# Work moved off ScalarE and VectorE in two attention layers: keys and values evicted by two engines, averages and edge columns on GpSimd, and a written-out ending

## The chip, the cores and the metric

The kernel runs on one core of a Trainium2 chip. The metric is the device time of one execution in microseconds, the median of three runs. The engines are named as in the profile: PE is TensorE's matrix multiplication and PEld its weight load, DVE is VectorE, ACT is ScalarE, POOL is GpSimd, and SP is SyncE, which here only issues DMAs. An "L" with a number is a line of the kernel before.

## What is computed

Four layers work in turn on `x` of shape (2, 128, 64, 64), all in fp32. The first is a sequence layer with a state-space scan, the second an attention with 3x3 convolutions for queries, keys and values; the change does not touch either. The third is an attention over all 4096 positions of each picture:

```python
q = einsum('dc,nci->ndi', wq, xf) + bq      # keys and values alike, with wk and wv
scores = einsum('nci,ncj->nij', q, k)
attn = softmax(scores, axis=-1)
out = einsum('ncj,nij->nci', v, attn)
return gamma[0] * out + x
```

The fourth is an attention between four scales of the same picture, at each position:

```python
for i, scale in enumerate((1, 2, 4, 8)):
    if scale > 1:
        xs = x.reshape(b, c, h//scale, scale, w//scale, scale).mean(axis=(3, 5))
        f = bilinear_resize(conv3x3(xs, conv_w[i], conv_b[i]), h, w)
    else:
        f = conv3x3(x, conv_w[i], conv_b[i])
# q, k, v of the 4 features; 8 heads of 16 channels; softmax over the 4 scales
res = (softmax(q k / 4) v) @ attn_out_w.T + attn_out_b + features
normed = (res - mu) * rsqrt(var + 1e-5) * ln_g + ln_b
out = einsum('bchw,oc->bohw', normed of the 4 scales, fus_w) + fus_b
```

## The kernel before, in words

The 128 channels lie on the partitions. The order of the instructions is written out by hand: each engine executes its instructions in the order of the code, and waits where an operand or a buffer is not ready. So an instruction that waits also holds up what is behind it on its engine.

**The attention layers.** One loop with a counter `now` runs over four "runs" of 128 steps, `runs = [(layer, batch)]`; runs 2 and 3 are the third layer of the network (called the second attention layer here). A run is processed in groups of 256 queries, `score` (L754, L759) writing the products of queries and keys `pq` into a pair of PSUM banks and copying them to SBUF while it takes their maximum, later steps of the same queue doing the exponential on ScalarE (L769), a transposition (L784 on DVE, then copies and DMAs to `pt`, L791 to L795) and the product with the values (`po`, L804). At step 0 of a run `keys` computes the 4096 keys in four chunks; at step 13 `values` does the same, and turns each chunk by eight TensorE transpositions (`turned`, `pvt` L714, copied by ScalarE at L716). In runs 2 and 3 `chunks` fills a pair of banks `pp` by two products (L683), and one ScalarE instruction, `put` (L592), adds the bias and writes the 1024 elements to SBUF. `pp` and `pq` share two buffers of two banks each. `query(r, 0)`, the first 256 queries, stands behind `keys`: a product `pqq` and a ScalarE `put`.

**The last layer.** There are 16 items, 8 of each batch, each of 512 positions by 4 scales. Its loop `period(n)` works on four items at once: the features of item n+2, the scores of item n+1, the weighting and mixing of item n, and the normalising and fusing of item n-1. In the order of the code a period has these steps:

- four slots, `ti` = 0 to 3. In each: `product` on DVE (L1157), `weights` on PE (`pw`, L1199), `scores` on PE (L1164), `weighted` on DVE (`ov`, L1206). In slot 0 also `normalise` (L1257) and `fuse` (`pfus`, L1264) of the item before; in slot 1 `add_ov` on POOL (L1210).
- two `add_ov` on DVE (L1210), the softmax on DVE and ACT (L1174 to L1192),
- `mix_out`: four times a pair of products `po` (L1219, L1220) and two ScalarE evictions, the square `sq` and the centred value `cen` (L1221, L1222),
- `variance` (`pva`, L1228, then three ScalarE instructions, L1233 to L1236), `newton` (`nt`, `rs`: DVE L1241, ACT L1242, DVE L1243), `factors` (`prs`, L1250), which spreads the result over the channels for the `normalise` of the next period.

`pw` and `prs` share one buffer of four PSUM banks; `psc`, `pva` and `pfus` share one bank; `po`, `pf`, `pqkv` and `pcs` share three.

`extra` places three things of a batch in slots of a period. `means` computes the averages of 2x2, 4x4 and 8x8 positions: two additions per scale on DVE (L1053, L1054), a `memset` on POOL (L1056), and ScalarE scales the sum into a padded tile (L1057). `coarse_conv` is the 3x3 convolution at that scale (`pcs`, L1069). `columns` interpolates along the rows: a difference `df` (L1085), two edge copies (L1088, L1089), one DVE instruction for each phase (L1092: 2, 4 and 8 of them), copies of the first and last row (L1095, L1096), and for the two coarser scales the difference of rows `di` (L1100). `features` builds the upsampled features of an item from them on POOL (L1124 to L1134). Batch 0 has them ahead of the loop. For batch 1, `means` stands behind the softmax of period 2, the convolutions in periods 3 and 4, and `columns` behind the softmax of period 5. The two last calls of the loop are period 15, in which only the old items have work, and period 16, which normalises and fuses item 15.

Of the kernel before, what the change touches and what calls it, by code (L numbers as in the profile page):

```python
# [6 lines left out]
F32 = mybir.dt.float32  # L7
AF = mybir.ActivationFunctionType
ALU = mybir.AluOpType
# [58 lines left out]
def tile_conv_seq(ctx: ExitStack, tc, x, consts, vecs, wemb, wlay, wconv, wdt, wqkv, wsmall, wms, out):  # L68
# [47 lines left out]
    with tc.manual_schedule(), ExitStack() as s:  # L116
# [474 lines left out]
        def put(dst, src, bias):  # L591
            nc.scalar.activation(dst, src, AF.Identity, bias=bias)  # L592

        def bias(r, which):
            return v1("b" + "qkv"[which] + "12"[runs[r][0]])
# [91 lines left out]
        def chunks(r, which, to):  # L687

            for cc in range(NCC):
                dst = to(cc)  # L690
                if runs[r][0]:
                    pp = pss.tile([P, 2, CH], F32, name="pp", tag="s")
                    for i in range(2):
                        dense(r, which, (2 * cc + i) * CH, CH, pp[:, i, :])
                    put(dst.rearrange("p (a f) -> p a f", a=2), pp, bias(r, which))
                else:
                    pp = products(which)
                    if cc + 1 < NCC:
                        fetch(cc + 1)
                    outputs(*pp, [dst[:, i * QG : (i + 1) * QG] for i in range(4)], bias(r, which))  # L700
# [36 lines left out]
        def query(r, grp):  # L737
            ps = psq.tile([P, QG], F32, name="pqq", tag="q")
            dense(r, 0, grp * QG, QG, ps)
            q = sta["q", r, grp] = spa.tile([P, QG], F32, name="q", tag="q", bufs=5)  # L740
            put(q, ps, bias(r, 0))
# [157 lines left out]
        for now in range(NALL + LAG + 10):  # L899
            r, u = divmod(now, NU)  # L900
            w = now % 8
            if now < NALL:
                if u == 0:
                    if r == 2:
                        wm = wbig.tile([P, NS, 9, C], F32, name="wm", tag="wbig")
                        nc.sync.dma_start(wm, wms)
                    if r:
                        keys(r)
                    if runs[r][0]:
                        query(r, 0)  # L910

                r4, cc = divmod((now + 16) // 32, NCC)
                v = (now + 16) % 32
                if now >= 16 and r4 < B:
                    if v == 0 and r4 and cc:
                        fetch(cc)
                    elif v == 0:
                        ahead = inputs(r4, cc)
                    if v < 6 and not (r4 and cc):
                        for f in ahead[2 * v : 2 * v + 2]:  # L920
                            f()
                    if v == 6 and r4 and cc == 0:
                        keep(0)
                    if v == 14:
                        queries(r4, cc)
                        if r4 and cc == 0:
                            load(1, HI)

                if r == 0 and u >= 32:
                    v = u % 32  # L930
                    if v == 0:
                        other = inputs(1, u // 32)
                    if v < 6:
                        for f in other[2 * v : 2 * v + 2]:
                            f()
                    if v == 6:
                        keep(u // 32)
                score(r, u)
                if runs[r][0]:
                    if w == 2 and u // 8 + 1 < NU // 8:  # L940
                        query(r, u // 8 + 1)
                elif u == 1 and r:
                    load(2, LO), load(2, HI)
                    fetch(0)
                elif u == LAG:
                    load(0, LO), load(0, HI)
                    if r == 0:
                        load(1, LO)
# [23 lines left out]
    with ExitStack() as s, tc.manual_schedule():  # L972
# [70 lines left out]


        def means(b):
            prev, off = xt[:, b], 1
            for si in range(1, NS):
                sc_ = SCALES[si]
                hh = H // sc_
                t1 = sp.tile([P, 2 * hh, hh], F32, name=f"t1_{si}", tag="prod", bufs=6)  # L1050
                sm = sp.tile([P, hh, hh], F32, name=f"sm_{si}", tag=f"fl{si}")
                e = off + 2 * hh
                nc.vector.tensor_tensor(t1, prev[:, off:e, off:e:2], prev[:, off:e, off + 1 : e : 2], ALU.add)  # L1053
                nc.vector.tensor_tensor(sm, t1[:, 0 : 2 * hh : 2, :], t1[:, 1 : 2 * hh : 2, :], ALU.add)  # L1054
                xs = coarse["xs", si] = sp.tile([P, hh + 2, hh + 2], F32, name=f"xs_{si}", tag=f"xs{si}")
                nc.gpsimd.memset(xs, 0.0)  # L1056
                nc.scalar.activation(xs[:, 1 : hh + 1, 1 : hh + 1], sm, AF.Copy, scale=1.0 / (sc_ * sc_))  # L1057
                prev, off = sm, 0

        def coarse_conv(si, r0):  # L1060
# [15 lines left out]
            else:  # L1076
                nc.scalar.activation(dst, src, AF.Identity, bias=v1("conv_b3", si))

        def columns(si):

            sc_ = SCALES[si]
            hh, half = H // sc_, sc_ // 2
            fl = coarse["fl", si]
            df = sp.tile([P, hh, hh - 1], F32, name=f"df_{si}", tag="prod", bufs=6)
            nc.vector.tensor_tensor(df, fl[:, :, 1:], fl[:, :, : hh - 1], ALU.subtract)  # L1085
            lo = sp.tile([P, hh + 2, W], F32, name=f"lo_{si}", tag=f"lo{si}")
            mid = lo[:, 1 : hh + 1, :]
            nc.vector.tensor_copy(mid[:, :, :half], fl[:, :, 0:1].to_broadcast([P, hh, half]))  # L1088
            nc.vector.tensor_copy(mid[:, :, W - half :], fl[:, :, hh - 1 : hh].to_broadcast([P, hh, half]))  # L1089
            for kk in range(half, half + sc_):  # L1090
                end = kk + sc_ * (hh - 2) + 1
                nc.vector.scalar_tensor_tensor(  # L1092
                    mid[:, :, kk:end:sc_], df, (kk + 0.5) / sc_ - 0.5, fl[:, :, : hh - 1], ALU.mult, ALU.add
                )
            nc.vector.tensor_copy(lo[:, 0, :], lo[:, 1, :])  # L1095
            nc.vector.tensor_copy(lo[:, hh + 1, :], lo[:, hh, :])  # L1096
            di = None
            if si > 1:
                di = sp.tile([P, hh + 1, W], F32, name=f"di_{si}", tag=f"di{si}")
                nc.vector.tensor_tensor(di, lo[:, 1:, :], lo[:, : hh + 1, :], ALU.subtract)  # L1100
            low[si] = lo, di


# [169 lines left out]
        def period(n, extra):  # L1273
# [49 lines left out]
                    do(p, newton)  # L1323
                do(r, project, 0, si)
            do(r, project, 1, 0)
            do(p, factors)
            do(r, project, 1, 1)
            more(6)

        means(0)  # L1330
        for r0 in (0, 16):
            coarse_conv(1, r0)
        coarse_conv(2, 0), coarse_conv(3, 0)
        for si in range(1, NS):
            columns(si)
        last = NCH - 3
        extra = {
            (last - 3, 4): [(means, (1,))],
            (last - 2, 1): [(coarse_conv, (1, 0))], (last - 2, 3): [(coarse_conv, (1, 16))],
            (last - 1, 1): [(coarse_conv, (2, 0))], (last - 1, 3): [(coarse_conv, (3, 0))],  # L1340
            (last, 4): [(columns, (si,)) for si in range(1, NS)],
        }
        for n in range(-2, NI + 1):
            period(n, extra)


# [79 lines left out]
```

## Time and profile before

| | |
|---|---|
| median of three runs | 5029.0 us (5028.12 to 5030.46) |
| the profiled execution's own time | 5032.79 us |
| its span, first to last instruction | 5031.0 us |
| granted TensorE clock, mean | 0.948 |
| PE busy | 4671.6 us, 93% of the span |
| DVE busy | 4024.3 us, 80% |
| ACT busy | 2367.4 us, 47% |
| POOL busy | 2309.9 us, 46% |
| keys of run 2 and 3 | from 3230.6 and about 3716 us |
| values of run 2 and 3 | to 3311.7 and 3795.7 us |
| last layer's regular period | 42.4 us from one `pva` to the next |
| last `weighted` to the end | 4995.75 to 5031.0 us |

The profile is of one execution, and every time stamp below is counted from the start of its span. Times of one instruction are from that execution too. In a timeline a line gives the start, the duration, the engine and line, the operation with its output and inputs, and in brackets how long the engine had been idle and what ended the idle time. ACTq and SPq are the DMA issues of these engines. In the list of waits a line gives the instruction that waited, the one that it waited for, the sum of the waits, how often, and the longest one.

### The profile page before, as it was taken

Reading aid. Unit: us, or ns where it says so; the run is one execution under the profiler, and the core shown is the slowest. Engines: PE = TensorE matmul, PEld = TensorE weight load, DVE = VectorE, ACT = ScalarE, POOL = GpSimd, SP = SyncE. Lnnn points to the kernel's source line nnn. Section 1 sums busy time; section 2 is a strip of 40 time slices with the busy share of each in tenths; the row PEclk is TensorE's granted clock in tenths of the full one; section 3 lists DMA queues with packets and bytes.
Section 4 is the critical chain, followed back from the end, with each engine's and each line's share of the span. In section 5 each row is a group of like instructions: output and inputs, shape, how many; then the busy total and the mean of one; then the engine's idle time right before and its main releaser. Section 6 shows DMA issues by size and latency. Waiting matters only on the chain.

```text
span 5031.0 us, 48923 instructions
## 1 busy us (share of the span) xinstructions
PE 4671.6 (93%) x14797; PEld 2244.9 (45%) x14797; DVE 4024.3 (80%) x4284; ACT 2367.4 (47%) x3221; POOL 2309.9 (46%) x1948
## 2 busy tenths in 40 slices
PE   5889999999988899899999999999999999999997
PEld 1222222222222222366667766666666666333332
DVE  6999999999999999788886677667766775767775
ACT  4677777777777777522222222333333332223332
POOL 3777776666777777513332233233333333323331
PEclk8898889988999989899999999999999999999998
DMA  6333333332333333224444344434443442000000
GB/s 162 68 68 69 69 71 71 71 68 63 71 68 68 72 71 70 62 65 108 109 110 126 105 112 110 117 98 110 114 100 97 112 111 70 5 5 7 7 7 7
DMA packets 242343, 386.24 MB, mean 77 GB/s; under 512 B 88592, under 2 KB 88992, under 8 KB 233632
## 3 DMA queue, kind: packets, MB, share of 16 engines
q1 hardware_dynamic: 192928, 315.94, 25.9%
q10 hardware_dynamic: 49152, 67.17, 5.4%
q8 instruction: 118, 1.93, 0.2%
q14 instruction: 145, 1.19, 0.1%
HBM read 101.02 MB, written 13.37 MB: 23 GB/s over the span
## 4 chain that ended last, share of the span: by engine, by line
PE 49%; POOL 24%; issue 12%; DVE 9%; ACT 2%; DMA 2%; SPq 1%; ACTq 0%; DVEq 0%; POOLq 0%
POOL h L410 19%; PE po L804 15%; PE pq L754 15%; PE pa L652 2%; PE pf L1113 2%; DVE tr L784 2%; PE pqkv L1140 2%; POOL dtu L370 1%; PE pw L1199 1%; POOL z L433 1%; PE pb L652 1%; PE pfus L1264 1%; PE psc L1164 1%; PE po L1220 1%; DVE prod L1157 1%
## 5 line engine op out<-in xcount | busy, mean ns | idle before, releaser
L791 POOL COPY pt<-tr 32x512 f32<-32x512 f32 x1024 | 649.0, 634 | 1440.2 <-DVE tr L784 711.7
L407 DVE TENSOR_TENSOR_SCAN h<-da,carry,h 128x512 f32<-128x512 f32 x1024 | 1241.6, 1266 | 59.9 <-ACT da L396 31.0
L410 POOL TENSOR_TENSOR h<-h,cb 128x2048 f32<-128x2048 f32 x256 | 1161.4, 4537 | 20.9 <-POOL carry L409 0.4
L754 PE MATMUL pq<-k,q 128*128 128x512 f32 x2048 | 962.8, 593 | 9.1 <-DVE sc L759 6.8
L804 PE MATMUL po<-pt,vt 128*128 128x256 f32 x4096 | 967.3, 379 | 2.8 <-DMA pt<-tr 2.8
L769 ACT ACTIVATE sc<-sc,nm 128x2048 f32<-128x2048 f32 x256 | 510.5, 1995 | 912.0 <-DVE nm L765 675.4
L759 DVE TENSOR_SCALAR_CACHE_REDUCE sc<-pq 128x1024 f32<-128x1024 f32 x512 | 625.0, 1222 | 366.7 <-PE pq L754 345.4
L804 PEld LDWEIGHTS po<-pt,vt 128*128 128x128 f32 x4096 | 779.1, 190 | 295.6 <-issue 208.3
L396 ACT ACTIVATE da<-dtb,am 128x512 f32<-128x512 f32 x1024 | 681.6, 684 | 231.1 <-DVE h L407 210.2
L389 DVE TENSOR_TENSOR h<-bb,pdu 128x2048 f32<-128x2048 f32 x256 | 581.8, 2273 | 85.8 <-PE py L422 29.3
L784 DVE STREAM_TRANSPOSE tr<-sc 128x2048 f32<-128x2048 f32 x256 | 591.7, 2311 | 63.2 <-DMA pt<-tr 53.9
L422 PE MATMUL py<-h,sel 128*32 128x512 f32 x2048 | 511.4, 643 | 1.6 <-POOL h L410 1.6
L754 PEld LDWEIGHTS pq<-k,q 128*128 128x128 f32 x2048 | 382.8, 190 | 284.8 <-issue 246.1
L383 PE MATMUL pdu<-dtu,fsel 128*128 128x512 f32 x512 | 325.3, 722 | 116.0 <-DVE h L389 113.8
L422 PEld LDWEIGHTS py<-h,sel 128*32 128x32 f32 x2048 | 115.2, 118 | 415.3 <-issue 409.9
L310 PE MATMUL pu<-xn,wu 128*128 128x512 f32 x512 | 246.7, 615 | 2.6 <-ACT xn L300 1.7
L383 PEld LDWEIGHTS pdu<-dtu,fsel 128*128 128x128 f32 x512 | 95.9, 214 | 321.8 <-DVE h L389 199.2
L409 POOL COPY carry<-h 128x4 f32<-128x4 f32 x256 | 47.5, 185 | 395.8 <-DVE h L407 393.9
L1206 DVE TENSOR_TENSOR ov<-v,pw 128x2048 f32<-128x2048 f32 x64 | 146.2, 2285 | 68.6 <-PE pw L1199 68.6
L1140 PE MATMUL pqkv<-f,ws 128*128 128x512 f32 x384 | 189.5, 618 | 3.0 <-DVE prod L1157 2.3
L1210 POOL TENSOR_TENSOR ov<-ov 128x2048 f32<-128x2048 f32 x16 | 72.6, 4536 | 257.7 <-DVE ov L1206 257.7
L370 POOL TENSOR_TENSOR dtu<-dt,u 128x1024 f32<-128x1024 f32 x32 | 75.1, 2346 | 191.9 <-ACT dt L364 191.9
(245 smaller groups left out, 5254.4 us busy)
## 6 DMA issues: line engine op xcount, KB each, us to landing
pt<-tr SPq DMA_DIRECT2D x2048, 64.0 KB, 2.0
dtb<-dt SPq DMA_DIRECT2D x1024, 64.0 KB, 2.0
pt<-tr ACTq DMA_DIRECT2D x1024, 64.0 KB, 2.2
bb<-dr SPq DMA_DIRECT2D x128, 256.0 KB, 4.4
cb<-dr SPq DMA_DIRECT2D x128, 256.0 KB, 4.7
uw<-ufold SPq DMA_DIRECT2D x12, 576.0 KB, 4.3
uw<-dkept SPq DMA_DIRECT2D x20, 288.0 KB, 3.0
xt<-in_x SPq DMA_DIRECT2D x16, 256.0 KB, 4.7
```

Of the source, the lines that this page charges most:

```text
L383: nc.tensor.matmul(pdu, lhsT=four(s_ % 4), rhs=st[i]["dtu"][:, s_ // 4, :], start=True, stop=True)
L389: nc.vector.tensor_tensor(h, st[i]["bc", 0], pdu.unsqueeze(1).to_broadcast([P, 4, CH]), ALU.mult)
L396: nc.scalar.activation(da, st[i]["dtb", s_], AF.Exp, scale=am[items[i][1]][:, j, gg, m : m + 1])
L407: nc.vector.tensor_tensor_scan(h[:, m, :], da, h[:, m, :], carries[b, l][:, j, gg, m : m + 1], ALU.mult, ALU.add)
L410: nc.gpsimd.tensor_tensor(h, h, st[i]["bc", 1], ALU.mult)
L422: nc.tensor.matmul(py[r : r + 32, :], lhsT=sel, rhs=st[i]["h", s_ + k][:, m, :], start=(m == 0), stop=(m == 3), tile_position=(0, r),)
L754: nc.tensor.matmul(pq[:, i, :], lhsT=sta["q", r, grp][:, it * P : (it + 1) * P], rhs=sta["k"][:, at : at + CH], start=True, stop=True)
L759: nc.vector.tensor_scalar(dst, pq, 1.0, None, ALU.mult, ALU.max, accum_out=sta["mx"][:, c2 : c2 + 1])
L769: nc.scalar.activation(sc, sc, AF.Exp, bias=nm, scale=scale, accum_out=sm[:, hh : hh + 1])
L784: nc.vector.transpose(tr, sta.pop(("sc", r, blk, hh)).rearrange("p (t r f) -> p r t f", r=NB, f=32))
L791: nc.gpsimd.tensor_copy(dst, src)
L804: nc.tensor.matmul(sta["po", r, grp], lhsT=sta["vt"][:, jt, :], rhs=rhs, start=(jt == 0), stop=(jt == N // P - 1))
```

## The change

It has four parts. In `chunks` the two banks of a pair are evicted by two instructions, the first by ScalarE and the second by VectorE (a `tensor_scalar` that adds the bias), both into the same destination tile; and the first queries of a run stand ahead of its keys. For batch 1, `means` is done on POOL in whole, with ScalarE's scaling too. `columns` is cut into three parts: for batch 1 the first (difference and edge copies) is done by POOL in slot 3 of period 5, the second (one instruction for each phase) by DVE behind the softmax, where all of it stood before, the third (edge rows and `di`) by POOL behind `mix_out`. And `ending` takes the place of periods 15 and 16: all the weighting of item 15 first, then the factors, normalising and fusing of item 14 (its factors stood in period 14 before), the additions with the last one cut in four by scale, the mixing of item 15, and its normalising cut in four by scale, each quarter with its fusing product.

```diff
@@ -692,7 +692,8 @@
                     pp = pss.tile([P, 2, CH], F32, name="pp", tag="s")
                     for i in range(2):
                         dense(r, which, (2 * cc + i) * CH, CH, pp[:, i, :])
-                    put(dst.rearrange("p (a f) -> p a f", a=2), pp, bias(r, which))
+                    put(dst[:, :CH], pp[:, 0, :], bias(r, which))
+                    nc.vector.tensor_scalar(dst[:, CH:], pp[:, 1, :], bias(r, which), None, ALU.add)
                 else:
                     pp = products(which)
                     if cc + 1 < NCC:
@@ -904,10 +905,10 @@
                     if r == 2:
                         wm = wbig.tile([P, NS, 9, C], F32, name="wm", tag="wbig")
                         nc.sync.dma_start(wm, wms)
+                    if runs[r][0]:
+                        query(r, 0)
                     if r:
                         keys(r)
-                    if runs[r][0]:
-                        query(r, 0)
 
                 r4, cc = divmod((now + 16) // 32, NCC)
                 v = (now + 16) % 32
@@ -1043,6 +1044,8 @@
 
 
         def means(b):
+
+            eng = nc.gpsimd if b else nc.vector
             prev, off = xt[:, b], 1
             for si in range(1, NS):
                 sc_ = SCALES[si]
@@ -1050,11 +1053,14 @@
                 t1 = sp.tile([P, 2 * hh, hh], F32, name=f"t1_{si}", tag="prod", bufs=6)
                 sm = sp.tile([P, hh, hh], F32, name=f"sm_{si}", tag=f"fl{si}")
                 e = off + 2 * hh
-                nc.vector.tensor_tensor(t1, prev[:, off:e, off:e:2], prev[:, off:e, off + 1 : e : 2], ALU.add)
-                nc.vector.tensor_tensor(sm, t1[:, 0 : 2 * hh : 2, :], t1[:, 1 : 2 * hh : 2, :], ALU.add)
+                eng.tensor_tensor(t1, prev[:, off:e, off:e:2], prev[:, off:e, off + 1 : e : 2], ALU.add)
+                eng.tensor_tensor(sm, t1[:, 0 : 2 * hh : 2, :], t1[:, 1 : 2 * hh : 2, :], ALU.add)
                 xs = coarse["xs", si] = sp.tile([P, hh + 2, hh + 2], F32, name=f"xs_{si}", tag=f"xs{si}")
                 nc.gpsimd.memset(xs, 0.0)
-                nc.scalar.activation(xs[:, 1 : hh + 1, 1 : hh + 1], sm, AF.Copy, scale=1.0 / (sc_ * sc_))
+                if b:
+                    nc.gpsimd.tensor_scalar(xs[:, 1 : hh + 1, 1 : hh + 1], sm, 1.0 / (sc_ * sc_), None, ALU.mult)
+                else:
+                    nc.scalar.activation(xs[:, 1 : hh + 1, 1 : hh + 1], sm, AF.Copy, scale=1.0 / (sc_ * sc_))
                 prev, off = sm, 0
 
         def coarse_conv(si, r0):
@@ -1076,28 +1082,35 @@
             else:
                 nc.scalar.activation(dst, src, AF.Identity, bias=v1("conv_b3", si))
 
-        def columns(si):
-
+        def columns(b, si, part):
+
+            eng = nc.gpsimd if b else nc.vector
             sc_ = SCALES[si]
             hh, half = H // sc_, sc_ // 2
             fl = coarse["fl", si]
-            df = sp.tile([P, hh, hh - 1], F32, name=f"df_{si}", tag="prod", bufs=6)
-            nc.vector.tensor_tensor(df, fl[:, :, 1:], fl[:, :, : hh - 1], ALU.subtract)
-            lo = sp.tile([P, hh + 2, W], F32, name=f"lo_{si}", tag=f"lo{si}")
-            mid = lo[:, 1 : hh + 1, :]
-            nc.vector.tensor_copy(mid[:, :, :half], fl[:, :, 0:1].to_broadcast([P, hh, half]))
-            nc.vector.tensor_copy(mid[:, :, W - half :], fl[:, :, hh - 1 : hh].to_broadcast([P, hh, half]))
-            for kk in range(half, half + sc_):
-                end = kk + sc_ * (hh - 2) + 1
-                nc.vector.scalar_tensor_tensor(
-                    mid[:, :, kk:end:sc_], df, (kk + 0.5) / sc_ - 0.5, fl[:, :, : hh - 1], ALU.mult, ALU.add
-                )
-            nc.vector.tensor_copy(lo[:, 0, :], lo[:, 1, :])
-            nc.vector.tensor_copy(lo[:, hh + 1, :], lo[:, hh, :])
+            if part == 0:
+                df = coarse["df", si] = sp.tile([P, hh, hh - 1], F32, name=f"df_{si}", tag="prod", bufs=6)
+                eng.tensor_tensor(df, fl[:, :, 1:], fl[:, :, : hh - 1], ALU.subtract)
+                lo = coarse["lo", si] = sp.tile([P, hh + 2, W], F32, name=f"lo_{si}", tag=f"lo{si}")
+                mid = lo[:, 1 : hh + 1, :]
+                eng.tensor_copy(mid[:, :, :half], fl[:, :, 0:1].to_broadcast([P, hh, half]))
+                eng.tensor_copy(mid[:, :, W - half :], fl[:, :, hh - 1 : hh].to_broadcast([P, hh, half]))
+                return
+            lo = coarse["lo", si]
+            if part == 1:
+                mid, df = lo[:, 1 : hh + 1, :], coarse.pop(("df", si))
+                for kk in range(half, half + sc_):
+                    end = kk + sc_ * (hh - 2) + 1
+                    nc.vector.scalar_tensor_tensor(
+                        mid[:, :, kk:end:sc_], df, (kk + 0.5) / sc_ - 0.5, fl[:, :, : hh - 1], ALU.mult, ALU.add
+                    )
+                return
+            eng.tensor_copy(lo[:, 0, :], lo[:, 1, :])
+            eng.tensor_copy(lo[:, hh + 1, :], lo[:, hh, :])
             di = None
             if si > 1:
                 di = sp.tile([P, hh + 1, W], F32, name=f"di_{si}", tag=f"di{si}")
-                nc.vector.tensor_tensor(di, lo[:, 1:, :], lo[:, : hh + 1, :], ALU.subtract)
+                eng.tensor_tensor(di, lo[:, 1:, :], lo[:, : hh + 1, :], ALU.subtract)
             low[si] = lo, di
 
 
@@ -1323,25 +1336,55 @@
                     do(p, newton)
                 do(r, project, 0, si)
             do(r, project, 1, 0)
-            do(p, factors)
+            if p != NI - 2:
+                do(p, factors)
             do(r, project, 1, 1)
             more(6)
+
+        def ending():
+
+            o, p = NI - 2, NI - 1
+            for ti in range(NS):
+                weights(p, ti)
+                weighted(p, ti)
+                if ti == 1:
+                    add_ov(nc.gpsimd, p, 0, 1)
+            factors(o)
+            normalise(o)
+            fuse(o, range(NS))
+            add_ov(nc.vector, p, 2, 3)
+            a, b = st[p]["ov", 0], st[p].pop(("ov", 2))
+            for si in range(NS):
+                nc.vector.tensor_tensor(a[:, si, :], a[:, si, :], b[:, si, :], ALU.add)
+            for si in range(NS):
+                mix_out(p, si)
+            variance(p)
+            newton(p)
+            factors(p)
+            w = st[p]
+            for si in range(NS):
+                nc.vector.tensor_tensor(w["cen"][:, si, :], w["cen"][:, si, :], w["prs"][:, si, :], ALU.mult)
+                fuse(p, (si,))
 
         means(0)
         for r0 in (0, 16):
             coarse_conv(1, r0)
         coarse_conv(2, 0), coarse_conv(3, 0)
         for si in range(1, NS):
-            columns(si)
+            for part in range(3):
+                columns(0, si, part)
         last = NCH - 3
         extra = {
             (last - 3, 4): [(means, (1,))],
             (last - 2, 1): [(coarse_conv, (1, 0))], (last - 2, 3): [(coarse_conv, (1, 16))],
             (last - 1, 1): [(coarse_conv, (2, 0))], (last - 1, 3): [(coarse_conv, (3, 0))],
-            (last, 4): [(columns, (si,)) for si in range(1, NS)],
+            (last, 3): [(columns, (1, si, 0)) for si in range(1, NS)],
+            (last, 4): [(columns, (1, si, 1)) for si in range(1, NS)],
+            (last, 5): [(columns, (1, si, 2)) for si in range(1, NS)],
         }
-        for n in range(-2, NI + 1):
+        for n in range(-2, NI - 1):
             period(n, extra)
+        ending()
 
 
 # ---- launch: one core ----
```

## The prediction

> **What bounds the kernel now.** I read the page's first line, then a table of busy time by stretch, the list of waits of the last stage, and the timelines around the places that the diff names.
>
> ```profile
> PE 4671.6 (93%) x14797; PEld 2244.9 (45%) x14797; DVE 4024.3 (80%) x4284; ACT 2367.4 (47%) x3221; POOL 2309.9 (46%) x1948
> ```
>
> TensorE is busy for 93% of the span. By stretch it is 543.62 of 560 us in 3230–3790 (a layer-2 attention run), 596.64 of 630 us in 4340–4970 (most of the last layer), but 43.64 of 71 us in 4960–5031. So a change pays where it closes a hole in TensorE, and elsewhere nearly not at all. What holes there are in 4340–4970, from the waits (total us, times, longest):
>
> ```profile
> PEld po L1219 <- ACT cen L1222: 7.7, 2, 7.5
> ...
> PE prs L1250 <- DVE rs L1243: 7.1, 1, 7.1
> ...
> PE po L1219 <- ACT cen L1222: 6.7, 1, 6.7
> ```
>
> Two holes, each once. Period starts tell what they cost: from one `pva` group to the next a regular period takes 42.4 us; the two periods with the holes take 51.1 and 51.6, so 8.7 and 9.2 us are lost. The first hole's timeline (start, duration, instruction, idle before it):
>
> ```profile
> 4406.53 4.62 DVE L1210 TENSOR_TENSOR ov<-ov 128x2048 f32<-128x2048 f32 x2
> ...
> 4417.05 2.25 DVE L1053 TENSOR_TENSOR t<-xt 128x2048 f32<-128x2048 f32 x1
> ...
> 4420.65 1.61 ACT L1057 ACTIVATE xs<-sm 128x1024 f32<-128x1024 f32 x2 [6.70 <-DVE sm L1054]
> ...
> 4423.89 2.07 PE L1219 MATMUL po<-f,kc 128*128 128x512 f32 x2 [6.68 <-ACT cen L1222]
> ```
>
> ScalarE stands at the scaling of `means(1)`, which needs VectorE's averages, and the evictions of `po` (L1221, L1222) queue behind it. The second hole and the lock beside it:
>
> ```profile
> 4585.43 0.61 POOL L1133 TENSOR_TENSOR f<-di,wgt 128x256 f32<-128x256 f32 x1 [1.56 <-DVE di L1100]
> 4585.48 0.60 DVE L1089 COPY lo<-fl 128x32 f32<-128x32 f32 x1
> ...
> 4589.69 0.68 DVE L1241 SCALAR_TENSOR_TENSOR nt<-pva,nt 128x512 f32<-128x512 f32 x1
> ...
> 4591.91 2.09 PE L1250 MATMUL prs<-rs,kc 32*128 32x512 f32 x8 [7.09 <-DVE rs L1243]
> ```
>
> Newton's `nt` was ready at 4582.1 (end of ACT L1236) and waits behind `columns` on VectorE, 4576.38 to 4589.77. The keys of run 2, and the tail:
>
> ```profile
> 3237.23 2.12 ACT L592 ACTIVATE k<-pp,vec 128x1024 f32<-128x1024 f32 x2 [2.34 <-DMA pt<-tr]
> 3238.39 6.11 PE L683 MATMUL pp<-xt,wa 128*128 128x512 f32 x8 [4.18 <-ACT k L592]
> 3244.55 1.11 ACT L592 ACTIVATE k<-pp,vec 128x1024 f32<-128x1024 f32 x1 [1.22 <-PE pp L683]
> 3245.56 0.47 ACT L592 ACTIVATE q<-pqq,vec 128x256 f32<-128x256 f32 x1
> 3246.08 1.98 PE L754 MATMUL pq<-k,q 128*128 128x512 f32 x4 [1.13 <-ACT q L592]
> ```
>
> ```profile
> 4975.04 2.09 PE L1250 MATMUL prs<-rs,kc 32*128 32x512 f32 x8 [4.30 <-DVE rs L1243]
> 4979.54 2.09 PE L1199 MATMUL pw<-at,spread 32*128 32x512 f32 x8 [2.41 <-DVE cen L1257]
> ...
> 5002.81 2.08 PE L1220 MATMUL po<-ov,wc 128*128 128x512 f32 x2 [5.12 <-DVE ov L1210]
> ```
>
> The tail is one chain PE, DVE, PE, with nothing beside it.
>
> **What the Trainium skill says.** "SBUF — State Buffer", section "SBUF: two separate sides": VectorE (two SBUF inputs, or a two-port mode) and a GpSimd operation that reads SBUF share a port pair under an exclusive lock; whichever starts first keeps it for the whole instruction and the other blocks. The trace agrees: the 32-element copies L1089 take 0.20 us alone, 0.60 above behind POOL's 0.61; the L1092 128x56 ones 0.25 alone and 0.77–0.80 when POOL runs; products with one operand in PSUM keep 2.29 us beside POOL's 4.54. "GPSIMD Engine Reference", section 3.1, states 4497 against 2293 ns for an addition of 2048 floats; the rows show 4537 (POOL L1210) and 2.29. "TensorE: Matmul & The Clock Gate", part 1: half clock after some 3.4 us idle. Here the L683 pitch is 0.43 us, and 0.86 after the 4.18 us hole.
>
> **The change part by part.** Nothing before 3230 us is touched. All sums are differences in the profiled execution (span 5031.0 us, execution 5032.79, 1.8 around the span); that execution is 3.8 above the median 5029.0, and I subtract from the median.
>
> *Keys and values of runs 2, 3.* Removed: an ACT eviction of 1.11 us per pair; added: ACT for one bank (0.69, as L1116) and VectorE for the other (0.69–0.73, as L1241 and L1174). VectorE is idle there (14.8 and 14.2 us before the first score). But in the built program VectorE's instruction waits for ScalarE's of the same pair, since both write one tile: 0.69+0.05+0.70 = 1.44 in series against 1.11. Keys: first query first, so q's put (0.47) goes before the keys; third pair at 3237.23+0.47+1.44 = 3239.13 instead of 3238.39 (+0.74); after the fourth pair, though, neither 0.60 of `pqq` nor q's put is left, and the first score needs only the keys' first part. The chain from the third pair to the score shrinks from 7.69 to about 5.9: first score 1.0 earlier. Values: the first `pvt` half reads bank 0 alone, so it starts after 0.69 instead of 1.11; following the four pairs through PE, ACT and DVE I get 1.1 of the 9.84 us (3301.83 to 3311.67). Twice both: 4.2. Bounds: if all 16 series costs lay on the path, 16×0.33 = 5.3 lost; if none, 6 gained. VectorE's values also wait for the tile's last transfers, issued 3304.4, 2.0 us to land, before it needs them.
>
> *Means of batch 1.* Removed: six VectorE sums (5.1 us) and ACT's 1.87 in front of `po`. Added on POOL, after its ov addition that ends 4401.62: 2048 sum 4.54, 1024 sum 2.35 (as L370), memsets 1.6, scaling of 1024 between 2 (as a two-operand row) and 3.4 (L1124's 0.86 per 256), small ones about 4: 15 us in all, needed by `coarse_conv` at about 4447. POOL's features behind it have slack: POOL idles 23.0 us before L1124. Without interference the period would be 42.4 and `pva` at 4418.86 for 4427.60. But the first sum ends at 4406.2 and the second runs 4406.28–4408.63, just where VectorE's two additions stood (4406.53–4411.15). Both sides alternate under the lock: additions end about 4415.4, softmax 4 us later, `pva` about 4421.8. Gain 5.8 to 6.0; bounds 3.5 (one more operation blocked) and 8.7.
>
> *Columns of batch 1.* Only the 14 scalar-tensor-tensors stay on VectorE in slot 4 (7.46 us in the trace); differences, edge copies and `di` (in all 5.9 of 13.4) go to POOL ahead and behind. `nt` runs at 4582.3–4584.8 instead of 4589.69, `prs` at 4584.8–4587.3 for 4591.91. The remaining wait is under 3.4 us, so the cold `prs` and `pw` (6.98 against 4.94) mostly go as well. Gain 7.0 of 9.2; bounds 5 and 9. POOL's chunk-8 features start later, covered by 40 us until used.
>
> *The ending.* `pw` of period 15 starts after `pva`(14), 4970.7, not at 4979.54; weighted 0 at 4975.04 (VectorE has just done newton), three more at 2.09+2.29+gaps: last ends 4990.9 for 4998.04. Then `prs`(14), 2.09, normalise 2.29, fuse to 5000.4 fill the time of VectorE's additions, which ended in the 5.12 hole. `po` runs warm 5000.4–5007.3 (8.76 before), `pva` to 5009.1, `prs`(15) 5013.6 for 5017.86: 4.3. Normalising by quarters: first `pfus` after 0.69 instead of 2.29, 1.6 more, the other quarters hidden under 0.86 of cold `pfus` each. Sum 6.0 to 6.2; bounds 4 (quarter waits) and 7.5.
>
> Sum: 4.2+6.0+7.0+6.2 = 23.4; 5029.0−23.4 = 5005.6, say 5006.
>
> **The rivals.** *No lock effect:* means 8.7 and columns 7.6 in full: 26.7, 5002. For it: the additions are long and may start first; against it: 0.60 for a 0.20 copy. *The split does not do what it says:* ACT and VectorE follow one another, so keys and values give 0 to +1: 5010. For it, the wait in the program; against it, the bank-0-only readers. *Lock worse:* POOL's scaling and copies dear and VectorE's 14 operations each held as at 0.8: means 2.5, columns 4: 5013, to 5018. *Slower:* POOL's first sum of `means` reads every second element of padded rows, a pattern that no POOL row shows. It holds the lock against L1210 from 4401.6, and from about 4407 each us more stalls TensorE one for one. The additions take 4.6 us after it: they end 8.7 late, at 4419.9, and the means' own gain is eaten, if the sum ends at 4415.3; another 17.4 later, at 4432.7, all gains are. So 31 us in place of 4.54 breaks even, and at 45 us the kernel takes 5043. Against it: POOL's L1124, every second row, costs 1.5 times per element of the 4.54 row, not 7 times.
>
> **How the numbers follow.** The forecast 0.60 (5001 to 5010), no lock 0.13, split worthless 0.10, lock worse 0.10, slow sum 0.07. What a measurement of this kernel tells from no change is 0.2%, 10 us: faster means under 5019. Faster 0.89 (all but part of the last two), same 0.07, slower 0.04. The range 4998 to 5015: upper bounds of the four (6+8.7+9+7.5 = 31) below, and the lock's dearer half above.
>
> **What would show it.** The first score of run 2 near 3245; VectorE's `k` puts right after ScalarE's. `pva` after means near 4417 (shifted by the 4.2), its period 45 instead of 51.1; L1210's additions longer than 2.3 us each there. The columns period near 44.5, `prs` hole under 3. In the tail no hole over 3 us before `po`, L1257 as four of 0.69. Wrong would be: a POOL sum far over 4.54, a hole at `pcs` behind POOL, or scores later than before.

## The result, and the profile after

The changed kernel takes 5006.53 us (median of five, 5004.69 to 5008.42) against 5030.46 us for the kernel before in the same session: ratio 0.9952, interval [0.9938, 0.9966], 23.9 us less. The profiled execution, the fastest of the five, has a span of 5002.9 us, 28.1 less than that of before. Line 1 of the page:

```profile
PE 4661.3 (93%) x14797; PEld 2242.4 (45%) x14797; DVE 4024.6 (80%) x4283; ACT 2358.8 (47%) x3218; POOL 2337.5 (47%) x1974
```

POOL is 28 us busier, and PE is busy for 10 us less with the same 14797 products: it ran at half clock less often (mean granted clock 0.950 for 0.948).

Stamps of the two traces, one place after the other, show where the 28.1 us are. A minus is time gained. The keys of a run begin with the first of its products, in the kernel after that of `query`. A "period" is the time from the `pva` before to its own.

| place | before | after | difference |
|---|---|---|---|
| up to the first product of run 2 | 3230.6 | 3230.2 | -0.4 |
| keys of run 2, first product to first score | 15.47 | 13.01 | -2.5 |
| from there to the first score after its values | 65.60 | 66.13 | +0.5 |
| keys of run 3 | 14.01 | 13.99 | 0.0 |
| to the first score after its values | 65.17 | 65.70 | +0.5 |
| from there to the first `pva` of the last layer | 538.3 | 536.2 | -2.1 |
| period of the averages, `pva` to `pva` | 51.1 | 42.7 | -8.4 |
| period of the columns | 51.6 | 42.4 | -9.2 |
| period 14 | 42.2 | 40.4 | -1.8 |
| last but one `pva` to the end | 62.1 | 57.4 | -4.7 |

The keys of run 2, with the query in front. Timeline of the kernel after (start, duration, instruction, idle before it):

```profile
3236.08 0.47 ACT L592 ACTIVATE q<-pqq,vec 128x256 f32<-128x256 f32 x1 [1.59 <-DMA pt<-tr]
3236.45 1.26 ACT L592 ACTIVATE k<-pp,vec 128x512 f32<-128x512 f32 x2
3237.16 1.41 DVE L696 TENSOR_SCALAR k<-pp,vec 128x512 f32<-128x512 f32 x2 [4.30 <-ACT k L592]
...
3237.97 5.40 PE L683 MATMUL pp<-xt,wa 128*128 128x512 f32 x8 [3.72 <-DVE k L696]
...
3243.21 1.88 PE L755 MATMUL pq<-k,q 128*128 128x512 f32 x4
```

VectorE's eviction waits for ScalarE's, as forecast, after an idle time of 4.30 us; the hole in PE is 3.72 us, hardly less than the 4.18 of before. The averages' place, timeline of the kernel after:

```profile
4401.42 2.35 POOL L1057 TENSOR_TENSOR sm<-t 128x1024 f32<-128x1024 f32 x1
...
4402.63 6.33 DVE L1223 TENSOR_TENSOR ov<-ov 128x2048 f32<-128x2048 f32 x2
...
4415.22 1.89 PE L1241 MATMUL pva<-sq,mean 128*32 128x512 f32 x8
```

VectorE's two additions take 6.33 us for 4.62: the lock is there, and costs 1.7 us on VectorE. But `pva` comes only 0.3 us late in its period. The columns:

```profile
4564.00 5.06 DVE L1104 SCALAR_TENSOR_TENSOR lo<-df,fl 128x992 f32<-128x992 f32 x14
...
4569.79 0.69 DVE L1254 SCALAR_TENSOR_TENSOR nt<-pva,nt 128x512 f32<-128x512 f32 x1 [0.72 <-ACT nt L1249]
...
4572.48 1.14 PE L1263 MATMUL prs<-rs,kc 32*128 32x512 f32 x8
```

`prs` is warm (1.14 us, not 2.09) and has no idle time in front. The ending:

```profile
4953.87 2.09 PE L1212 MATMUL pw<-at,spread 32*128 32x512 f32 x8 [5.43 <-DVE ov L1219]
...
4967.37 2.09 PE L1263 MATMUL prs<-rs,kc 32*128 32x512 f32 x8 [2.41 <-DVE ov L1219]
...
4971.87 6.06 PE L1277 MATMUL pfus<-cen,wfus 128*128 128x512 f32 x8 [2.41 <-DVE cen L1270]
...
4993.91 5.29 PE L1277 MATMUL pfus<-cen,wfus 128*128 128x512 f32 x8 [0.80 <-DVE cen L1366]
```

The order is the planned one, but both `pfus` groups run mostly at half clock, 6.06 and 5.29 us, where a warm group (one at full clock) takes 3.60.

### The profile page after: what moved, and what is told of

Same layout as the page of the kernel before. It is cut to its first block, busy times and chain, and to the rows that moved or that the text cites. A ratio compares the mean times of both kernels' runs of the same rounds, so it can differ in the third digit from the quotient of the medians.

```text
span 5002.9 us, 48954 instructions
## 1 busy us (share of the span) xinstructions
PE 4661.3 (93%) x14797; PEld 2242.4 (45%) x14797; DVE 4024.6 (80%) x4283; ACT 2358.8 (47%) x3218; POOL 2337.5 (47%) x1974
## 5 line engine op out<-in xcount | busy, mean ns | idle before, releaser
L407 DVE TENSOR_TENSOR_SCAN h<-da,carry,h 128x512 f32<-128x512 f32 x1024 | 1241.6, 1266 | 59.7 <-ACT da L396 30.7
L1219 DVE TENSOR_TENSOR ov<-v,pw 128x2048 f32<-128x2048 f32 x64 | 146.2, 2285 | 62.1 <-PE pw L1212 62.1
```

Of the source, the lines that this page charges most:

```text
L407: nc.vector.tensor_tensor_scan(h[:, m, :], da, h[:, m, :], carries[b, l][:, j, gg, m : m + 1], ALU.mult, ALU.add)
```

## The experiments

**Each part alone.** Four kernels, each the kernel before with one part of the change; the theory was by then that the averages and columns give their whole loss back and the keys and values nearly nothing.

First part alone (both diff hunks of `chunks` and of the query):

> Only the first part of the change: two engines evict, first query first; the last layer is as before. The prediction's sum says 4.2 us faster, 5025 against 5029. The two profiles in hand say less: run 2's keys gained 2.5 us, run 3's keys nothing, and both values lost 0.6 us, because the first transpositions and the product behind them run on a half-speed clock there; so about 1 us faster, and the same slow products at both values. If the split were worth nothing and the query's place all, the trace would show keys shorter and values longer by about 0.6 us again.

5027.21 us, ratio 0.9989 [0.9981, 0.9997]. Keys of run 2 took 11.34 us, of run 3 13.99; from there to the score after the values 64.54 and 65.70. So one values stage gained 1.1 us and the other lost 0.5, as both do in the kernel after: the expectation of slow products in both was wrong. Sum of the four differences: 4.7 us gained, for 1.4 in the changed kernel, though this part is the same in both. The second half of run 2's keys in this kernel:

```profile
3235.80 3.72 PE L683 MATMUL pp<-xt,wa 128*128 128x512 f32 x8 [3.73 <-DVE k L696]
```

The hole is that of the changed kernel (3.72), but its eight products took 5.40 us there. The first transpositions and products of run 2's values, in this kernel and then in the kernel after:

```profile
3295.85 1.44 PE L715 MATMUL pvt<-kc,vs 128*128 128x128 f32 x8 [2.38 <-ACT vs L592]
3297.12 1.89 PE L683 MATMUL pp<-xt,wa 128*128 128x512 f32 x4
```

```profile
3299.60 1.64 PE L715 MATMUL pvt<-kc,vs 128*128 128x128 f32 x8 [2.38 <-ACT vs L592]
...
3301.03 3.42 PE L683 MATMUL pp<-xt,wa 128*128 128x512 f32 x4
```

The same program, the same hole of 2.38 us, and four products take 1.89 or 3.42 us: the clock. Its granted share is 1.00 in 3295.85 to 3299.2 here, and 0.53 in 3301.03 to 3304.29 of the kernel after. So in one profile a single stage can be 1.7 us off by the clock alone.

Averages alone, columns alone, ending alone:

> Only the averages of batch 1 on GpSimd, with their scaling. Theory (lock cost hidden): the period that took 51.1 us takes 42.4 to 42.8 us, so 8.4 us and perhaps a little more from a warm clock afterwards; VectorE's two ov additions there take about 3.3 and 3.0 us instead of 2.31. Rival (the prediction): 45.3 us, 5.9 us gained.

5023.39 us, 0.9984 [0.9978, 0.9991]. The period takes 42.7 us, VectorE's additions 3.30 and 3.01. The theory held, the prediction's 45.3 did not.

> Only the edge columns of batch 1 in three parts. Theory: the period that took 51.6 us takes 42.4, 9.2 us gained, no hole before prs there. Rival (the prediction): 44.6 us, 7.0 us gained. In both the averages' hole of 6.7 us before po stays.

5023.35 us, 0.9983 [0.9976, 0.9990]. The period takes 43.7 us: between the two values. The timeline shows why (of this kernel, alone with the columns changed):

```profile
4580.83 3.17 DVE L1101 SCALAR_TENSOR_TENSOR lo<-df,fl 128x56 f32<-128x56 f32 x5
...
4581.26 2.49 POOL L1110 TENSOR_TENSOR di<-lo 128x1088 f32<-128x1088 f32 x1
...
4583.88 0.68 DVE L1251 SCALAR_TENSOR_TENSOR nt<-pva,nt 128x512 f32<-128x512 f32 x1
```

One of the 128x56 operations started at 4581.30, 0.04 us after POOL's `di`, and took 2.57 us where its neighbours take 0.25 to 0.30: the whole of `di`. In the changed kernel POOL's copy in front of `di` took 0.88 us, so that `di` came after VectorE's last one. One race for the lock, 1.3 us; the kernel without the split, below, lost it too (2.57 us again, and a period of 43.7).

> Only the written-out ending. From the last but one pva to the end the kernel before took 62.15 us. The prediction says about 56.0 us; the profile after showed 57.4 us, with fuse of item 14 at half clock (6.06 us). Expected here: 57.4 us, 4.7 us gained.

5026.79 us, 0.9989 [0.9983, 0.9996]; the tail took 58.2 us, 3.9 gained where the two profiles had said 4.7. The four ratios together say 0.55% or 27.7 us; all parts in one kernel 0.48%. Within their intervals the parts add up.

**The first part taken apart.**

```diff
@@ query_first, against the kernel before
+                    if runs[r][0]:
+                        query(r, 0)
                     if r:
                         keys(r)
-                    if runs[r][0]:
-                        query(r, 0)
@@ split_only, against the kernel before
-                    put(dst.rearrange("p (a f) -> p a f", a=2), pp, bias(r, which))
+                    put(dst[:, :CH], pp[:, 0, :], bias(r, which))
+                    nc.vector.tensor_scalar(dst[:, CH:], pp[:, 1, :], bias(r, which), None, ALU.add)
```

> Of the first part only the place of the first queries; one ScalarE instruction evicts a pair as before. Theory (the values' loss comes from the split): both values keep 8.67 us from the first transposition to the next score, as in the four kernels without the split, and no half-speed stretch lies there; keys of run 2 near 14.4 us from their first product to the first score (15.5 before: one put of 0.47 is added in front, pqq and the put behind go), of run 3 near 13. Rival (the place of the query makes the difference in the values by shifting the clock's windows): values at 9.7 us or 8.05 here too.

> Of the first part only the two evictions; the first queries stay behind the keys. Theory: values take 8.05 us from the first transposition to the next score where the clock stays full, 9.73 where a half-speed stretch of 3.4 us falls on them (8.67 before); keys gain nothing, 15 to 16 us in run 2 and 14 to 15 in run 3, since the pair costs 1.44 us in series for 1.11. In time: within 2 us of the kernel before.

5029.04 us, 0.9997 [0.9988, 1.0006], and 5028.77 us, 0.9995 [0.9986, 1.0004]: neither differs from the kernel before.

| | keys run 2 | run 3 | to the score after values, run 2 | run 3 | sum of differences |
|---|---|---|---|---|---|
| before | 15.47 | 14.01 | 65.60 | 65.17 | |
| query first | 13.39 | 12.63 | 66.88 | 66.46 | -0.9 |
| split | 14.92 | 15.09 | 64.54 | 65.44 | -0.3 |

The theory that the split makes the values slow is refuted: with the query alone moved, both values stages run into half clock (10.06 and 10.08 us from the first transposition to the next score; 8.68 before). Nor does the query decide it alone: with the split, one of two stages has it. What they share is *when* the hole begins. The half-clock records of one trace (the stretches for which it notes a granted clock of 0.5) begin at whole multiples of 3.413 us from one another (488.1 us between those in the keys of run 2 and of run 3 in the kernel before is 143 of them), and they lie where the products are slow: 3300.7 to 3304.1 for the stage with 3.42 us above. I took that grid in each run, with its points at the records' own stamps. There are 24 values stages in the twelve kernels with a hole of 2.38 to 2.82 us ahead of the first transposition. Where the hole began between 0.36 us before a grid point and 0.98 us behind one, a half-clock stretch followed, 14 of 14; where it began 1.42 to 2.44 us behind one, none, 10 of 10. (The expectation of `no_split` below gives such places counted from another zero.) In the first group most or all of the hole falls into one window of the grid, in which PE is idle for 2.26 to 2.81 us, and the next window is at half clock; in the second it is shared between two windows, and PE is idle for 1.99 us at most in either. This is no threshold for the whole kernel: in the kernel before a window near 4936 with 1.86 us of idle time is followed by half clock too.

The stages of the four profiles with the old keys and values (before, and the averages, columns and ending alone) lay in the good group all eight times; in the kernels that move the keys by a microsecond or two, 14 of the 16 values stages some 66 us later lay in the bad one. So the gain of 1.1 us at equal clock, forecast for the split, is there (64.54), and a loss of about 1.7 us (9.73 against 8.05 from transposition to score) hides it where the clock falls. "TensorE: Matmul & The Clock Gate" in the Trainium skill, part 1, calls the window free-running and of 3413 ns; the grid of these runs agrees, though the hole here is shorter than one window.

The same, I think, explains the 2.1 us between 3795 and 4330 and the 1.8 us of period 14, where the change touches nothing but the place of one group of products. In the first, before has half-clock stretches of 3.4, 10.2 and 3.4 us (from 4216, 4233 and 4308), after of 6.8 and 3.4 (from 4233 and 4304). In period 14 time and clock go together in all fourteen profiles: 42.2 us in the five with two stretches of 3.4 us, 42.0 in the five with one, 40.4 in the four with none. These four, the changed kernel among them, are of the eight kernels that have the factors out of it. This is read from the traces; no run changed the clock by itself.

**What lengthens VectorE's additions.** Changed kernel, but the scaling of the averages back on ScalarE:

```diff
-                if b:
-                    nc.gpsimd.tensor_scalar(xs[:, 1 : hh + 1, 1 : hh + 1], sm, 1.0 / (sc_ * sc_), None, ALU.mult)
-                else:
+                if True:
                     nc.scalar.activation(xs[:, 1 : hh + 1, 1 : hh + 1], sm, AF.Copy, scale=1.0 / (sc_ * sc_))
```

> The changed kernel, but ScalarE scales the averages of batch 1 and GpSimd only adds. It tells what lengthens VectorE's two ov additions, 3.29 and 3.01 us in the changed kernel. Theory: the first waits for the second sum, which stays, so 3.2 to 3.3 us again; the second for GpSimd's scaling, which is gone, so 2.3 us. The period of the averages stays at 42.4 to 42.7 us, as ScalarE's three copies are ready before the mixing now. Rival (both engines merely slow each other by memory traffic): the second stays near 3.0.

One execution, 5010.8 us. Timeline of this kernel:

```profile
4405.37 6.35 DVE L1221 TENSOR_TENSOR ov<-ov 128x2048 f32<-128x2048 f32 x2
...
4407.49 2.08 POOL L1056 TENSOR_TENSOR t<-sm 128x512 f32<-128x512 f32 x1
...
4409.65 2.66 POOL L1057 TENSOR_TENSOR sm<-t 128x256 f32<-128x256 f32 x1
...
4414.55 1.50 ACT L1061 ACTIVATE xs<-sm 128x1024 f32<-128x1024 f32 x3
```

The second addition kept its 3.01 us, so the 2.3 expected without the scaling was wrong: POOL's next sums come forward and stand in its way. They show the lock from the other side: 2.08 and 2.66 us where the same sums take 1.33 and 0.73 in the changed kernel. The rival is not settled by this, nor what lengthens the second addition in the changed kernel. There POOL does this beside it:

```profile
4404.86 3.70 POOL L1061 TENSOR_SCALAR xs<-sm 128x1024 f32<-128x1024 f32 x1
```

Had the addition waited until this scaling ended at 4408.56, it could not have ended at 4408.96; what it waited for stays open. And the period grew to 43.9 us; ScalarE's copies stand behind the exponential again and in front of the mixing's evictions. By this one execution, moving the scaling to POOL is worth 1.2 us of the averages' gain.

**Place or engine.** Changed kernel, all of the columns on VectorE, at the new places, the third part behind the factors:

```diff
-            eng = nc.gpsimd if b else nc.vector
+            eng = nc.vector
-            (last, 5): [(columns, (1, si, 2)) for si in range(1, NS)],
+            (last, 6): [(columns, (1, si, 2)) for si in range(1, NS)],
```

> The changed kernel, but VectorE does all three parts of batch 1's columns at their new places, the third behind the factors. Rival (the place does it, not GpSimd): 42.4 us as in the changed kernel. Theory (VectorE must be rid of the work): the first part, 1.15+0.60+0.21 and edge copies, 3.2 us in all, stands ahead of the ov additions, and the third, 3.3 us, ahead of the next product, so this period and the next are longer by 3 to 6 us together.

One execution, 5015.14 us; the period took 48.8 us for 42.4, its neighbours 0.5 and 0.2 more: 7.1 us lost, a little more than the 3 to 6 expected, as `normalise` comes late and PE cools:

```profile
4584.59 2.09 PE L1212 MATMUL pw<-at,spread 32*128 32x512 f32 x8 [3.89 <-DVE cen L1270]
```

So it is mostly POOL, not the order, that brings the columns' gain: by this one execution 7.1 of the 9.2 us, with the third part one step later than in the changed kernel.

**Better versions.** First, the changed kernel without the split; then with VectorE evicting whole pairs:

```diff
@@ no_split
+                    put(dst.rearrange("p (a f) -> p a f", a=2), pp, bias(r, which))
@@ pairs_by_dve
+                    nc.vector.tensor_scalar(dst.rearrange("p (a f) -> p a f", a=2), pp, bias(r, which), None, ALU.add)
@@ both in place of
-                    put(dst[:, :CH], pp[:, 0, :], bias(r, which))
-                    nc.vector.tensor_scalar(dst[:, CH:], pp[:, 1, :], bias(r, which), None, ALU.add)
```

> The changed kernel with the pair of banks evicted by ScalarE alone again; the query stays in front. If the split is worth what it saves (0.6 us in each values stage at equal clock, nothing in the keys), this is within 2 us of the changed kernel, 0.9948 to 0.9960 of the kernel before. In both values stages the half-speed stretch falls or not by where the hole begins in the clock's grid of 3.41 us: in the runs so far it fell when it began 1.66 to 3.20 us after a grid point, and not at 0.16 to 1.45.

5003.82 us, 0.9946 [0.9934, 0.9959]: not told apart from the changed kernel, 0.9952 in its own session. The split is worth nothing that can be measured in the time.

> The changed kernel, but VectorE evicts each whole pair of the keys and values of runs 2 and 3, with one instruction of 128x1024 (1.22 us, as its evictions of scores). Theory: what delays the keys is not the eviction's length but that ScalarE is busy with exponentials and DMA issues until 3236, while VectorE idles from 3233; so the hole of 3.7 us in the keys goes, and the first score comes 6.4 to 8 us after the first product, not 13 to 14: 5 to 7 us gained in each run. Values: their buffers are those of the transposes, whose DMAs land late, so the hole there stays and they gain nothing. Together 10 to 14 us faster than the changed kernel, about 0.993 of before. Rival (ScalarE's length of eviction was the limit): no gain, as 1.22 is longer than 1.11.

4987.40 us, 0.9910 [0.9895, 0.9925], 19 us faster than the changed kernel had been, and more than expected. Timeline, keys and then values of run 2:

```profile
3232.48 7.18 PE L683 MATMUL pp<-xt,wa 128*128 128x512 f32 x16
...
3234.65 1.25 DVE L695 TENSOR_SCALAR k<-pp,vec 128x1024 f32<-128x1024 f32 x1
...
3236.25 1.64 ACTq L793 DMA_DIRECT2D pt<-tr  x2
3237.93 0.47 ACT L592 ACTIVATE q<-pqq,vec 128x256 f32<-128x256 f32 x1 [1.59 <-PE pp L683]
...
3239.50 1.88 PE L754 MATMUL pq<-k,q 128*128 128x512 f32 x4
```

```profile
3292.45 2.45 ACTq L793 DMA_DIRECT2D pt<-tr  x4
3292.65 1.26 DVE L695 TENSOR_SCALAR vs<-pp,vec 128x1024 f32<-128x1024 f32 x1
3293.97 1.09 PE L714 MATMUL pvt<-kc,vs 128*128 128x128 f32 x8 [0.46 <-DVE vs L695]
```

All sixteen passes of the keys run without a hole and warm, and VectorE evicts the first pair while ScalarE still works at exponentials and issues DMAs. Keys take 7.45 and 7.42 us, 5.6 and 6.6 less than in the changed kernel, and the values' stretch is 3.7 and 3.1 us shorter. There I was wrong: the hole of 2.38 us before the first transposition was not the buffers' late DMAs but ScalarE's own queue. In the changed kernel the eviction follows ScalarE's DMA issues, of which this is the last:

```profile
3298.00 0.60 ACTq L794 DMA_DIRECT2D pt<-tr  x1
3298.86 0.69 ACT L592 ACTIVATE vs<-pp,vec 128x512 f32<-128x512 f32 x1 [6.38 <-POOL pt L792]
```

VectorE evicts beside the same four issues. The hole is 0.46 us here, and 1.17 in run 3, and no half-clock stretch follows either. Part of the gain is that: by an estimate from the durations above, about 8 of the 19 us are half clock that no longer falls (eight products of 5.40 and 6.37 us in the keys for 3.60 warm, and 1.7 in each values stage).

**Another ending.** The changed kernel with the core of the ending rewritten. `o` is item 14 and `p` item 15, `w` the state of `o`; `spread_out` does the work of `weights` and `weighted` in four single banks; the second group of dots stands for the addition in four parts, the third for the four products of item 14's `pfus`. `newton` of item 14 leaves period 14, and `cen` of item 15 gets a buffer of its own:

```diff
+            def spread_out(ti):
+                banks = [mmt("pw1") for _ in range(NS - 1)] + [pac.tile([P, CH], F32, name="pw1", tag="acc")]
...
+                for si in range(NS):
+                    nc.vector.tensor_tensor(ov[:, si, :], v, banks[si], ALU.mult)
+            weights(p, 0)
+            weighted(p, 0)
+            nc.vector.scalar_tensor_tensor(w["nt"], w.pop("pva"), LN_EPS, w["nt"], ALU.add, ALU.mult)
+            nc.scalar.activation(w["nt"], w["nt"], AF.Identity, bias=c15, scale=-0.5)
+            spread_out(1)
+            nc.vector.tensor_tensor(w["rs"], w["rs"], w["nt"], ALU.mult)
+            add_ov(nc.gpsimd, p, 0, 1)
+            weights(p, 2)
+            weighted(p, 2)
+            spread_out(3)
+            factors(o)
+            add_ov(nc.vector, p, 2, 3)
...
+            normalise(o)
+            for si in range(NS):
+                mix_out(p, si)
+            variance(p)
+            w["pfus"] = mmt("pfus")
...
+            newton(p)
+            factors(p)
```

> The changed kernel with another ending: item 15's weights go alternately to the usual four banks and to four others, so that TensorE fills one set while VectorE reads the other; newton of item 14 stands behind the first weighting; the additions and the mixing of item 15 go ahead of normalising and fusing item 14, which then fill its wait for the variance. Theory: the end is one chain of item 15, and the weighting costs 4 times 4.48 us only since one set of banks is shared; 2 times 2.3 plus 2 times 2.8 plus newton's 1.4 instead: from the last but one pva to the end about 43 us, not 57.4, 13 to 15 us gained, about 0.9925 of before. Rival (VectorE bounds the ending): under 6 us.

4988.02 us, 0.9911 [0.9897, 0.9924]; the tail takes 40.6 us for 57.4, 16.8 gained.

```profile
4956.29 2.47 DVE L1359 TENSOR_TENSOR ov<-v,pw 128x512 f32<-128x512 f32 x4
4956.43 2.09 PE L1263 MATMUL prs<-rs,kc 32*128 32x512 f32 x8 [0.68 <-DVE ov L1219]
...
4961.94 2.08 PE L1233 MATMUL po<-ov,wc 128*128 128x512 f32 x2 [1.42 <-DVE ov L1375]
...
4971.99 3.70 PE L1382 MATMUL pfus<-cen,wfus 128*128 128x512 f32 x8
...
4978.40 3.70 PE L1277 MATMUL pfus<-cen,wfus 128*128 128x512 f32 x8 [0.80 <-DVE cen L1390]
```

The weighting ends 11.6 us after `pva`'s end (4947.2 to 4958.8) instead of 19.9, item 14's fusing fills the wait for the variance, and both `pfus` run warm: 3.70 us each. The rival, VectorE as the bound, falls. The second set of banks, the moved `newton` and the new order came in together; this run does not tell what each is worth.

> The changed kernel with both: VectorE evicts the pairs, and the reordered ending. The two places are 700 us apart and share nothing, so the gains add: 23 to 29 us beyond the changed kernel, 4978 to 4984 us, about 0.990 of before.

4970.39 us, 0.9877 [0.9863, 0.9890]: 61.5 us less than the kernel before beside it, 36 less than the changed kernel had taken, and 8 below the least I expected, since each of the two gave more than expected: 19.1 and 18.5, which add up to 37.6.

## Why the prediction was right or wrong

The time was right, 5006.5 for 5006, and the direction and the four places too. That the number came so close is luck: of the four terms in its sum none was within a microsecond of what its place gave, and they made up for each other (23.4 us forecast, 23.7 measured in the four places).

- **Keys and values: 4.2 forecast, 1.4 in the changed kernel (4.7 in the kernel with this part alone).** The step that failed is "following the four pairs through PE, ACT and DVE I get 1.1": it took warm products. At warm clock it was exact (65.60 to 64.54). Left out was that half-clock stretches fall by the grid. The keys, forecast at 1.0 in each run, gained 2.5 and nothing (4.1 and nothing in the kernel with this part alone), again with the clock: the eight products behind their hole took 5.40 and 6.37 us (3.72 and 6.39). The rival that the split does nothing came out for the split itself: without it the kernel is as fast. That both write one tile was given as the reason of the wait; no run shows the reason, only the wait.
- **The averages: 6.0 forecast, 8.4.** The lock came as the forecast said, its size did not. The additions ended 1.7 us late, not 4.3; the first sum took 3.65 us, where the 4.54 of another row had been taken, so that the second met only the start of the additions. And of those 1.7 us the period showed 0.3: the prediction passed 2.9 of its 4.3 us on to `pva`, far too large a share.
- **The columns: 7.0 forecast, 9.2 (7.9 where POOL's `di` wins the lock).** The 7.46 us for fourteen operations, read from the trace of before, contained VectorE's waits for POOL's features there: beside a POOL that does little but edge copies they take 5.06. A duration read beside a contended lock is not a price.
- **The ending: 6.2 forecast, 4.7 and 3.9.** The order and the stamps up to the last weighting were as worked out (21.8 us after `pva`, 22.0 forecast); the two terms of its sum, 4.3 and 1.6, make 5.9 and not the 6.0 to 6.2 given. The mis-sized term is `fuse`: 6.06 us for some 5.1; the last one took 5.29. PE is busy for 58% of this tail, and 30.7 of its 57.4 us are at half clock.
- **The slow rival** (a POOL sum of 31 us or more) found nothing: the strided sum took 3.65 us, less than the plain row. (The rival with a worse lock adds up to 5012, not 5013, and VectorE's 128x56 operations beside a running POOL took 0.69 to 0.79 us, not 0.77 to 0.80; nothing hangs on either.)
- **Unforeseen:** 2.1 and 1.8 us in unchanged places, most likely the clock. They are in the two profiled executions, one 2.3 us above its median and the other 1.8 below; the median moved by 23.9, not 28.1.

What the forecast did not see at all is that keys and values had 20 us to give. It priced evictions, 1.11 against 1.44, and took as given that ScalarE starts them at 3237; the wait that ended last there was for ScalarE's queue.

## What to carry to other kernels

When an eviction is late, ask first why its engine starts late, and only then how long it takes: a longer instruction on an idle engine (1.25 us on VectorE for 1.11 on ScalarE) was worth 19 us, two shorter ones in series nothing. Take durations from places where the shared port was free, and pass a delay on only as far as the next wait has no slack. A small shift ahead of a hole of 2.4 us can change TensorE's clock behind it by more than the shift is worth, so look for the same stage in several runs before believing half a microsecond.

## What the runs showed of the hardware

TensorE's half-clock records keep a grid of 3.413 us within a run. A hole of 2.38 to 2.82 us in the values was followed by a half-clock stretch where 2.26 us or more of idle time fell into one window of that grid, and by none where at most 1.99 did (24 of 24 stages, as told above). The lock between VectorE and POOL is decided by hundredths of a microsecond: 0.04 us made a 0.25 us operation take 2.57.
